# Scan operands of a four-layer image kernel: first pieces given inside the tick, later pieces one by one, last chunks' sums together

## The chip, the cores and the metric

The kernel runs on one core of a Trainium2 chip. The metric is the device time of one execution in microseconds (us); the lower, the better. Engines are named as in the profile: PE (TensorE matmul) and PEld (its weight load), DVE (VectorE), ACT (ScalarE), POOL (GpSimd) and SP (SyncE, which issues nearly all DMAs here). L12 is line 12 of the kernel before.

## The reference

`x` has the shape (4, 128, 64, 64): four images of 128 channels and 4096 pixels, float32. Four layers follow one another, each with a residual and a group norm of 32 groups in front:

```
x = x + attention(_gn(x))         # softmax attention over the 4096 pixels
x = x + radial_conv5x5(_gn(x))    # 128 -> 128 channels
x = x + selective_scan(_gn(x))    # the layer of this change
x = x + conv3x3(_gn(x))           # 128 -> 128 channels
```

The scan layer projects its input with Wx. It takes one half of the channels forwards and the other half backwards over the pixels. On each half it does:

```
xc    = silu(causal depthwise conv, 4 taps)
delta = softplus(xc @ Wd + bd);  Bm = xc @ WB;  Cm = xc @ WC
h[t]  = exp(delta[t] * A) * h[t-1] + (delta[t] * xc[t]) * Bm[t]    # 64 states per channel
y[t]  = sum over states(h[t] * Cm[t]) + D * xc[t]
```

The two halves are joined and projected with Wp.

## The kernel before

**Two streams in one order.** No scheduler moves instructions: each engine runs its instructions in the order in which the program gives them. One Python loop, `scan_core` (L1431), gives the recurrence in 1024 ticks: 256 for each of the four images, in four chunks of 1024 pixels, two directions, 16 groups of four states and two groups of channels. The other stream, `images` (L1781), is a chain of generators: load, attention, 5x5 convolution and scan operands of each image, and later the ends and the 3x3 convolutions. After each half tick the loop runs pieces of this second stream until the costs that they yield (0.7 for a `SLOT`, 0.86 for a `PRODUCT`) have used up the image's pace, so many units to a tick (`PACES`, L47). While image b is in the recurrence, the second stream makes image b+1. Before an image's first tick the loop runs the second stream without limit until the operands of its first chunk are there (`before`). For image 0 there is no recurrence to run beside, so its front stands alone.

**A tick.** In iteration i, POOL multiplies `db` for tick i+2 (`drive`, L1535), ACT makes the decay `da` of tick i+1 (`decay`, L1528), DVE scans tick i (`recur`, L1545), and the product with C, `hc`, is made on DVE (L1548) or for some ticks on POOL (`weigh`, L1566). `to_pool` gives POOL one product in three in the wide state, three of five while the operands of the next image are made ("operands" in `ready`), and one in five in the last part of that ("drives" in `ready`). PE adds the states up (L1584). SP loads the rows `br` and `cr` and the steps `dx` and `de` four ticks ahead, or up to eight at the start of an image.

**Wide and narrow.** Usually the decay of a tick is one instruction of 1024 elements into one of two double PSUM banks. While scan operands are made, these banks belong to the bank `s2` and three half banks. Decay and scan are then two instructions of 512 elements each. `widen` changes over when "narrow" is added to or taken from `ready`; the end of the 5x5 convolution adds it, the end of the scan operands takes it away.

**Scan operands of an image.** `Sums.settle` (L359) turns sums into scale and shift: small operations on DVE, and then two on POOL (L376, L377). In front of the scan it waits for the next tick (`next_tick`) before those two. `scan_prep` (L1240) clears the edges of the padded image `xn` on POOL (L1247, L1248), normalises its first and last piece of 512 pixels on ACT (`piece`, through L424), and hands over to `scan_operands` (L1263). That has a table of slots. For chunk i, at slot 5i + ...:

| slot | what | engine |
| --- | --- | --- |
| 0, 1 | `taps`: depthwise conv and Wx in 16 products (L1284) | PE |
| 4 | `halves`: half of it, and tanh (L1299, L1306; image 0 has the first on DVE, L1301) | ACT |
| 5 | `silu` (L1310), and the write of `xcd` | DVE, SP |
| 8, 9, 12 | `delta_product`, `row_product` 1 and 2 (L1319) | PE |
| 10 | `softplus`, its linear part (L1333, L1334) | ACT |
| 11, 13 | `row` 1 and 2: copies for B and C (L1325), and their writes | ACT, SP |
| 12 | `exp` (L1362, L1368) | ACT |
| 13 | `digits` (L1339, L1340) | DVE |

After chunk 3 and after chunk 7 (in image 0 after chunks 1, 5 and 7) come the logarithms of the chunks so far (`logs`, L1375), the additions that finish delta (`join`, L1347, and the write of `dd`), and delta times xc (`drives`, L1352, and the write of `dxd`). The additions run on POOL, or on DVE where the logarithm went to a PSUM bank: chunks 4, 5 and 6 of images 1 to 3. Slot 0 also normalises pieces 1 and 6, slot 1 pieces 2 and 5, slot 2 pieces 3 and 4. "read" at slot 2 lets the next image's load begin, ten turns later. After image 3's operands, `last_weights` (L917 to L920) prepares the weights of the last convolution on DVE.

**The next image beside it.** `both` runs an image's operands and the `start` of the image that follows it in turn, one piece of each. Its key products (`keys`, L477) begin after "taps" at slot 39.

Of the kernel before, what the change touches and what calls it, by code (L numbers as in the profile page):

```python
# [27 lines left out]
ALU = mybir.AluOpType  # L28
# [15 lines left out]


PRODUCT, VALUES, HOP, SLOT, AHEAD, EARLY = 0.86, 0.9, 1.7, 0.7, 4, 8
PACES = 2.60, 2.57, 2.57, 1.55  # L47


BQ, BK, BX, BP, CONVB, BD, DSKIP, MAINB, CONVW, ALOG = 0, 1, 2, 3, 4, 5, 6, 7, 8, 12  # L50
# [3 lines left out]
def conv_preact_kernel(  # L54
# [16 lines left out]
    nc = tc.nc  # L71
    B, C, H, W = x.shape
    L = H * W
# [7 lines left out]
    NM = L // MM  # L81
# [10 lines left out]
    pools, ready = {}, set()  # L92
    more = None

    def bank(tag, name):
        return pools.get(tag, ps).tile([P, MM], F32, tag=tag, name=name)
# [233 lines left out]
    class Sums:  # L330
# [25 lines left out]

            self.away, self.begun = other.minus, True

        def settle(self, name, wait=False):  # L359

            def cell(tag):
                return small.tile([P, 1], F32, tag=f"gn_{tag}", name=f"{tag}_{name}")

            total = small.tile([P, 2], F32, tag="gn_total", name=f"total_{name}")
            nc.vector.tensor_reduce(total, self.sums, AX.X, ALU.add)
            mean, power = self.spare[:, 0:1], self.spare[:, 1:2]
            nc.tensor.matmul(self.spare[:, 0:2], gmean, total, start=True, stop=True)
            off, less, var, rs, nb = (cell(tag) for tag in ("off", "less", "var", "rs", "nb"))
            minus = self.minus = small.tile([P, 1], F32, tag=f"gn_mi{name[0]}", name=f"mi_{name}")
            nc.vector.tensor_scalar(off, mean, self.away, -1.0, ALU.add, ALU.mult)  # L370
            nc.vector.scalar_tensor_tensor(less, mean, self.away, off, ALU.add, ALU.mult)
            nc.vector.scalar_tensor_tensor(var, less, GN_EPS, power, ALU.add, ALU.add)
            nc.vector.tensor_scalar(minus, mean, -1.0, None, ALU.mult)
            if wait:
                yield from next_tick()
            nc.gpsimd.tensor_tensor(rs, var, mhalf, ALU.pow)  # L376
            nc.gpsimd.tensor_tensor(nb, minus, rs, ALU.mult)  # L377
            return rs, nb

    def next_tick():  # L380

        begun = ticks_begun[0]
        while begun and ticks_begun[0] == begun:
            yield 0.4
# [38 lines left out]
    def normalise(dst, src, gn):  # L423
        nc.scalar.activation(dst, src, AF.Identity, scale=gn[0], bias=gn[1])  # L424
# [27 lines left out]
    def attention_start(b, xn):  # L452

        if b == 0:
            st = stats_tile(f"a{b}")
            for i in range(NM):
                nc.vector.bn_stats(st[:, i, :], xn[:, bass.ts(i, MM)])
                yield 0.0
            gn = yield from group_norm(st, f"a{b}")
        while b > 0 and (b - 1, "taps") not in ready:  # L460
            yield 0.0
        v = pools["big"].tile([P, VSIZE], F32, tag="V", name=f"v_{b}")
        v = v[:, : NJT * (C + 1)].rearrange("p (j c) -> p j c", c=C + 1)
        nc.gpsimd.memset(v[:, :, C : C + 1], 1.0)
        pvs = {}

        def piece(i):
            cut = bass.ts(i, L // 4)
            if b == 0:
                normalise(xn[:, cut], xn[:, cut], gn)  # L470

        def keys(i):

            tag = "saz"[i % 3] if b == 0 else "s" if i < 3 or i % 2 == 0 else "s2" if "s2" in pools else "z"
            pvs[i] = bank(tag, f"pv_{b}_{i}").rearrange("p (t c) -> p t c", c=C)
            for t in range(TPM):
                nc.tensor.matmul(  # L477
                    pvs[i][:, t, :], xn[:, bass.ts(i * TPM + t, P)], wv, start=True, stop=True
                )

        def take(i):
            nc.scalar.copy(v[:, i * TPM : (i + 1) * TPM, :C], pvs.pop(i))

        piece(0)
        yield SLOT
        for i in range(NM):
            if i % 2 == 0 and i // 2 + 1 < 4:
                piece(i // 2 + 1)
            keys(i)
            yield SLOT  # L490
            if b > 0:
                take(i)
                yield 0.0
            elif i > 0:
                take(i - 1)
        if b == 0:
            take(NM - 1)
        return xn, v
# [741 lines left out]
    def scan_prep(b, xs, st, mats4):  # L1240


        bc, dd, dxd, xcd, xsd = mats4
        pad = KC - 1
        gn = yield from st.settle(f"s{b}", True)
        xn = pools["big"].tile([P, VSIZE], F32, tag="V", name=f"xn2_{b}")
        nc.gpsimd.memset(xn[:, :pad], 0.0)  # L1247
        nc.gpsimd.memset(xn[:, pad + L : 2 * pad + L], 0.0)  # L1248

        def piece(*chunks):  # L1250
            for i in chunks:
                cut = slice(i * MM, (i + 1) * MM)
                normalise(xn[:, pad + cut.start : pad + cut.stop], xs[:, cut], gn)
            for i in {i // 2 for i in chunks if i % 2}:
                nc.sync.dma_start(xsd[:, bass.ts(i, CH)], xs[:, bass.ts(i, CH)])

        piece(0)
        piece(NM - 1)
        while "wide" in pools:
            yield HOP  # L1260
        return scan_operands(b, xn, mats4, piece)

    def scan_operands(b, xn, mats4, piece):  # L1263
# [78 lines left out]
        def join(c):  # L1342
            for i in range(c * CH // MM, (c + 1) * CH // MM):
                cut = bass.ts(i, MM)

                eng = nc.vector if b > 0 and NM // 2 <= i < NM - 1 else nc.gpsimd
                eng.tensor_tensor(delta[:, cut], delta[:, cut], us.pop(i), ALU.add)  # L1347
            nc.sync.dma_start(dd[c], delta[:, bass.ts(c, CH)])

# [20 lines left out]
        def logs(i, j):  # L1370
            for n in range(i, j):
                to = us[n]
                if b > 0 and j == NM and n - i < 3:
                    to = bank(("a", "z", "s2")[n - i], f"ln_{b}_{n}")
                nc.scalar.activation(to, us[n], AF.Ln)  # L1375
                us[n] = to

# [7 lines left out]
        def at(slot, f, *args):  # L1385
            slots.setdefault(slot, []).append((f, args))

        for i in range(NM):
            t = EVERY * i
            at(t, taps, i, 0, 1)  # L1390
            at(t + 1, taps, i, 2, 3)
            at(t + 4, halves, i)
            at(t + 5, silu, i)
            at(t + 8, delta_product, i)
            at(t + 9, row_product, i, 1)
            at(t + 10, softplus, i)
            at(t + 11, row, i, 1)
            at(t + 12, exp, i)
            at(t + 12, row_product, i, 2)
            at(t + 13, digits, i)  # L1400
            at(t + 13, row, i, 2)

        PER = CH // MM
# [1 line left out]
        for i, j in zip(cuts, cuts[1:]):  # L1405
            t = EVERY * (j - 1) + 15
            at(t, logs, i, j)
            for n, c in enumerate(range(i // PER, j // PER)):
                at(t + 1 + n, join, c)
                at(t + 3 + n, drives, c)  # L1410
                at(t + 4 + n, ready.add, (b, "operands", c))
        at(0, piece, 1, NM - 2)
        for n in range(2, NM // 2):
            at(n - 1, piece, n, NM - 1 - n)
        at(2, ready.add, (b, "read"))
        at(EVERY * (NM - 1) + 4, ready.add, (b, "taps"))
        at(EVERY * (NM - 1) + 13, ready.add, "drives")
        ready.add("operands")
        for t in range(max(slots) + 1):
            for f, args in slots.get(t, ()):  # L1420
                f(*args)
            yield SLOT
        ready.discard("operands")
        ready.discard("drives")
        ready.discard("narrow")
# [5 lines left out]
    def scan_core(mats4, ynds, before, widen, result):  # L1431
# [194 lines left out]
        def do(step, i, *args):  # L1626
            if 0 <= i < n:
                step(i, *args)

        for i in range(-AHEAD, n + 4):  # L1630
            if (i + AHEAD) % TICKS == 0 and i + AHEAD < n:
                before((i + AHEAD) // TICKS)
            do(drive, i + 2)
            ticks_begun[0] = i + AHEAD + 1 if i < n + 3 else 0
            do(keep, i - 1)
            late = i + 1 < n and i >= 0 and widen()
            if not late:
                do(decay, i + 1, 0)
            do(recur, i)
            if late:  # L1640
                do(keep, i)
                late()
                do(decay, i + 1, 0)
            do(weigh, i - 1)
            if i < n + 3:
                do(take, i - 4)
            do(preset, i - 4)
            do(collect, i - 3)
            yield i
# [20 lines left out]
    def program(safe):  # L1670
# [26 lines left out]
        def front(b, xn, v):  # L1697
# [21 lines left out]
            ynds[b] = dram.tile([NM, P, MM], F32, tag="ynd", bufs=B, name=f"ynd_{b}")  # L1719
            operands = yield from scan_prep(b, xs, st2, mats4[b])  # L1720
            if b + 1 < B:
                return (yield from both(operands, start(b + 1, 10)))
            yield from operands
            last_weights()

# [229 lines left out]
```

## Time and profile before

| | |
| --- | --- |
| time before, median of 3 runs | 4182.58 us (4182.18 to 4189.49) |
| the profiled execution | 4187.43 us |
| its span, first to last instruction | 4184.1 us |
| busy: PE, DVE, ACT, POOL | 3687.0, 3514.0, 2325.1, 3525.7 us |
| granted clock of PE, mean | 0.934 |
| first scan starts, last scan ends | 685.3 us, 4118.4 us |
| first scan of images 1, 2, 3 | 1559.4, 2429.4, 3307.8 us |
| narrow ticks | 0 to 7, 242 to 259, 497 to 514, 752 to 768 |

A busy engine in this table is busy over the whole span. A group's line in the profile gives its busy time, the mean of one instruction in ns, and the engine's idle time before such instructions with what ended it. A line of a timeline gives start, duration, engine, line, operation, output and inputs, and in square brackets the idle time before it. A line of the list of waits gives who waited for whom, the sum in us, the number of times and the longest.

### The profile page before, as it was taken

Reading aid. Unit: us, or ns where it says so; the run is one execution under the profiler, and the core shown is the slowest. Engines: PE = TensorE matmul, PEld = TensorE weight load, DVE = VectorE, ACT = ScalarE, POOL = GpSimd, SP = SyncE. Lnnn points to the kernel's source line nnn. Section 1 sums busy time; section 2 is a strip of 40 time slices with the busy share of each in tenths; the row PEclk is TensorE's granted clock in tenths of the full one; section 3 lists DMA queues with packets and bytes.
Section 4 is the critical chain, followed back from the end, with each engine's and each line's share of the span. In section 5 each row is a group of like instructions: output and inputs, shape, how many; then the busy total and the mean of one; then the engine's idle time right before and its main releaser. Section 6 shows DMA issues by size and latency. Waiting matters only on the chain. (4 is left out here: it accounts for less than half of the span.)

```text
span 4184.1 us, 49830 instructions
## 1 busy us (share of the span) xinstructions
PE 3687.0 (88%) x17668; PEld 2140.8 (51%) x17668; DVE 3514.0 (84%) x2441; ACT 2325.1 (56%) x3900; POOL 3525.7 (84%) x1688
## 2 busy tenths in 40 slices
PE   8999997999999979999999889999998576675856
PEld 4444443778875327887763368787733121221212
DVE  3842215999999979999999899999998899999996
ACT  3344306667665476766664676666645654545442
POOL 2433315999999979999999799999998899999995
PEclk9999998999999989999999999999999788797877
DMA  1020006555555666555555575555655756666661
GB/s 66 31 104 26 3 11 239 196 191 191 195 190 190 192 240 222 197 192 194 192 190 193 203 253 195 191 197 185 204 179 197 258 199 230 205 213 224 211 234 61
DMA packets 223728, 740.99 MB, mean 177 GB/s; under 512 B 29662, under 2 KB 30942, under 8 KB 223212
## 3 DMA queue, kind: packets, MB, share of 16 engines
q1 hardware_dynamic: 221548, 736.99, 52.0%
q8 instruction: 140, 2.29, 0.2%
q14 instruction: 120, 0.98, 0.1%
q10 hardware_dynamic: 1920, 0.73, 0.1%
HBM read 662.14 MB, written 75.47 MB: 176 GB/s over the span
## 5 line engine op out<-in xcount | busy, mean ns | idle before, releaser
L1535 POOL TENSOR_TENSOR db<-dx,br 128x1024 f32<-128x1024 f32 x1024 | 2398.5, 2367 | 119.4 <-DVE hc L1545 44.6
L1528 ACT ACTIVATE da<-de,a_neg 128x1024 f32<-128x1024 f32 (+1 forms) x1085 | 1160.3, 1070 | 375.2 <-DVE hc L1548 272.6
L1545 DVE TENSOR_TENSOR_SCAN da<-da,last,db 128x1024 f32<-128x1024 f32 (+1 forms) x500 | 1152.8, 2306 | 21.7 <-ACT last L1561 10.6
L1548 DVE TENSOR_TENSOR hc<-da,cr 128x1024 f32<-128x1024 f32 (+1 forms) x698 | 824.7, 1182 | 61.8 <-issue 1.3
L1566 POOL TENSOR_TENSOR hc<-hc,cr 128x1024 f32<-128x1024 f32 x354 | 837.4, 2366 | 6.8 <-ACT last L1561 3.6
L1584 PE MATMUL y<-hc,sel 128*32 128x512 f32 x4096 | 601.3, 649 | 270.2 <-POOL hc L1566 206.9
L748 PEld LDWEIGHTS acc<-v,exchange 128*128 128x128 f32 x6144 | 799.7, 191 | 48.3 <-issue 10.6
L727 PE MATMUL sc<-r,x 128*128 128x256 f32 x3072 | 803.0, 386 | 21.2 <-ACT exchange L740 16.2
L748 PE MATMUL acc<-v,exchange 128*128 128x129 f32 x6144 | 803.3, 275 | 1.5 <-ACT exchange L740 1.5
L727 PEld LDWEIGHTS sc<-r,x 128*128 128x128 f32 x3072 | 527.9, 191 | 188.5 <-ACT exchange L740 41.2
L1545 DVE TENSOR_TENSOR_SCAN hc<-da,last,db 128x1024 f32<-128x1024 f32 (+1 forms) x268 | 597.3, 2229 | 7.0 <-ACT last L1561 3.6
L740 ACT ACTIVATE exchange<-sc 128x512 f32<-128x512 f32 x768 | 441.8, 588 | 171.9 <-PE sc L727 164.6
L1584 PEld LDWEIGHTS y<-hc,sel 128*32 128x32 f32 x4096 | 113.6, 113 | 620.6 <-POOL hc L1566 303.4
L1545 DVE TENSOR_TENSOR_SCAN da<-da,db 128x1024 f32<-128x1024 f32 (+1 forms) x170 | 376.6, 2215 | 14.9 <-ACT da L1528 10.5
L1561 ACT COPY last<-da 128x1 f32<-128x1 f32 x511 | 80.4, 157 | 542.9 <-DVE hc L1548 541.9
L549 POOL TENSOR_TENSOR sidep<-sidep,exchange 128x512 f32<-128x512 f32 x120 | 165.0, 1375 | 254.3 <-ACT exchange L531 251.9
L531 ACT ACTIVATE exchange<-sc 128x512 f32<-128x512 f32 x256 | 152.6, 596 | 254.5 <-PE sc L530 246.5
L549 DVE TENSOR_TENSOR sided<-sided,exchange 128x512 f32<-128x512 f32 x120 | 98.5, 821 | 214.7 <-ACT exchange L531 213.6
L537 PE MATMUL acc<-exchange,v 128*128 128x512 f32 x512 | 261.9, 594 | 0.9
L530 PE MATMUL sc<-r,x 128*128 128x512 f32 x512 | 262.1, 594 | 0.6 <-ACT r L513 0.6
L893 PE MATMUL pcm<-xpm,cs 128*128 128x512 f32 x432 | 213.0, 643 | 10.3 <-ACT xpm L424 10.3
L1545 DVE TENSOR_TENSOR_SCAN hc<-da,db 128x1024 f32<-128x1024 f32 (+1 forms) x86 | 190.7, 2218 | 7.6 <-ACT da L1528 5.1
(295 smaller groups left out, 3048.6 us busy)
## 6 DMA issues: line engine op xcount, KB each, us to landing
br<-bm SPq DMA_DIRECT2D x512, 512.0 KB, 4.0
cr<-cm SPq DMA_DIRECT2D x512, 512.0 KB, 4.6
dx<-dxd SPq DMA_DIRECT2D x64, 512.0 KB, 5.3
de<-dd SPq DMA_DIRECT2D x64, 512.0 KB, 6.3
xs<-in_x_dram SPq DMA_DIRECT2D x16, 512.0 KB, 6.0
xsd<-xs SPq DMA_DIRECT2D x16, 512.0 KB, 5.2
xcd<-xc SPq DMA_DIRECT2D x16, 512.0 KB, 2.6
bm<-bs SPq DMA_DIRECT2D x32, 256.0 KB, 5.4
```

The lines of the kernel that those rows point to most:

```text
L530: nc.tensor.matmul(sc, xn[:, bass.ts(j, P)], rq[blk], start=True, stop=True)
L537: nc.tensor.matmul(acc[blk], v[:, j, :C], ring[:, u % NRING, :], start=j == 0, stop=j == NJT - 1)
L549: eng.tensor_tensor(s, s, ring[:, u % NRING, :], ALU.add)
L727: nc.tensor.matmul(sc[:, bass.ts(n, HM)], xn[:, bass.ts(2 * k + n, P)], rq[blk][:, cut], start=True, stop=True,)
L740: nc.scalar.activation(pt, sc, AF.Exp)
L748: nc.tensor.matmul(acc[part][:, bass.ts(t, CV)], ring[:, u % NRING, n * HM + t * P : n * HM + (t + 1) * P], v[:, 2 * k + n, :], start=(k, ...
L1528: nc.scalar.activation(da, rep["de", b, c, d, g][:, bass.ts(h, size)], AF.Exp, scale=a_neg[:, at(i)])
L1535: nc.gpsimd.tensor_tensor(dbs[i], rep["dx", b, c, d, g], rows["b", b, c, d, q], ALU.mult)
L1545: nc.vector.tensor_tensor_scan(h, da, db[:, cut], before, ALU.mult, ALU.add)
L1548: nc.vector.tensor_tensor(hc[:, cut], h, rows["c", b, c, d, q][:, cut], ALU.mult)
L1566: nc.gpsimd.tensor_tensor(hcs[i], hcs[i], rows["c", b, c, d, q], ALU.mult)
L1584: nc.tensor.matmul(y[r : r + SG, :], sel, hcs[first + gg][:, bass.ts(h, MM)], start=False, stop=q == NQ - 1, tile_position=(0, r), skip_gr ...
```

## The change

- `settle` takes a function instead of a flag. The two operations on POOL, and that function after them, are put on a list of hooks. The loop runs the list inside the next tick, behind its `drive` and ahead of its `decay` and `recur`. The function clears the edges of `xn` and normalises pieces 0 and 7. Without a running recurrence the list is run at once.
- The other six pieces get slots of their own: piece 1 at slot 2 and 6 at 3, 2 at 6 and 5 at 7, 3 at 11 and 4 at 12. "read" comes at slot 13 instead of 2, and the next image's load five turns after it instead of ten.
- `silu` moves from slot 5 to 6 of a chunk and `digits` from 13 to 14.
- At the last logarithms (slot 50), all additions are at slot 51, and the drives at 52 and 53. Slots after 50 yield no cost: there is one wait for the next tick after slot 50, and all that is left is given together.
- Two instead of three of the last logarithms go to PSUM banks (`a`, `z`; no longer `s2`), so chunk 6 is added on POOL. Odd key products use bank `s` while operands are made and `z` afterwards.
- The paces of images 1, 2 and 3 go from 2.57, 2.57, 1.55 to 2.56, 2.55, 1.53.

```diff
-PACES = 2.60, 2.57, 2.57, 1.55
+PACES = 2.60, 2.56, 2.55, 1.53
...
-        def settle(self, name, wait=False):
+        def settle(self, name, then=None):
...
-            if wait:
-                yield from next_tick()
-            nc.gpsimd.tensor_tensor(rs, var, mhalf, ALU.pow)
-            nc.gpsimd.tensor_tensor(nb, minus, rs, ALU.mult)
+
+            def finish():
+                nc.gpsimd.tensor_tensor(rs, var, mhalf, ALU.pow)
+                nc.gpsimd.tensor_tensor(nb, minus, rs, ALU.mult)
+                if then:
+                    then((rs, nb))
+
+            if then:
+                hooks.append(finish)
+                while hooks and ticks_begun[0]:
+                    yield 0.4
+                run_hooks()
+            else:
+                finish()
             return rs, nb
...
-            tag = "saz"[i % 3] if b == 0 else "s" if i < 3 or i % 2 == 0 else "s2" if "s2" in pools else "z"
+            tag = "saz"[i % 3] if b == 0 else "s" if i % 2 == 0 or "operands" in ready else "z"
...
-        piece(0)
-        piece(NM - 1)
+        def first(gn):
+            scale_shift.append(gn)
+            nc.gpsimd.memset(xn[:, :pad], 0.0)
+            nc.gpsimd.memset(xn[:, pad + L : 2 * pad + L], 0.0)
+            piece(0)
+            piece(NM - 1)
+
+        yield from st.settle(f"s{b}", first)
...
-                eng = nc.vector if b > 0 and NM // 2 <= i < NM - 1 else nc.gpsimd
+                eng = nc.vector if b > 0 and NM // 2 <= i < NM - 2 else nc.gpsimd
...
-                if b > 0 and j == NM and n - i < 3:
-                    to = bank(("a", "z", "s2")[n - i], f"ln_{b}_{n}")
+                if b > 0 and j == NM and n - i < 2:
+                    to = bank("az"[n - i], f"ln_{b}_{n}")
...
-            at(t + 5, silu, i)
+            at(t + 6, silu, i)
...
-            at(t + 13, digits, i)
+            at(t + 14, digits, i)
...
-                at(t + 1 + n, join, c)
-                at(t + 3 + n, drives, c)
-                at(t + 4 + n, ready.add, (b, "operands", c))
-        at(0, piece, 1, NM - 2)
-        for n in range(2, NM // 2):
-            at(n - 1, piece, n, NM - 1 - n)
-        at(2, ready.add, (b, "read"))
+                at(t + (1 if j == NM else 1 + n), join, c)
+                at(t + (2 if j == NM else 3) + n, drives, c)
+                at(t + (2 if j == NM else 4) + n, ready.add, (b, "operands", c))
+        for n in range(1, NM // 2):
+            at(EVERY * (n - 1) + 1 + (n == 1), piece, n)
+            at(EVERY * (n - 1) + 2 + (n == 1), piece, NM - 1 - n)
+        at(EVERY * (NM // 2 - 2) + 3, ready.add, (b, "read"))
...
-            yield SLOT
+            if t <= EVERY * (NM - 1) + 14:
+                yield SLOT
+            elif t == EVERY * (NM - 1) + 15:
+                yield from next_tick()
...
             ticks_begun[0] = i + AHEAD + 1 if i < n + 3 else 0
+            run_hooks()
             do(keep, i - 1)
...
-                return (yield from both(operands, start(b + 1, 10)))
+                return (yield from both(operands, start(b + 1, 5)))
```

More of the change, by code (lines that the diff above doesn't have):

```diff
@@ L373, in settle, with run_hooks @@
             nc.vector.tensor_scalar(minus, mean, -1.0, None, ALU.mult)
-            if wait:
-                yield from next_tick()
-            nc.gpsimd.tensor_tensor(rs, var, mhalf, ALU.pow)
-            nc.gpsimd.tensor_tensor(nb, minus, rs, ALU.mult)
+            def finish():
[10 more added lines that the diff above has]
+                finish()
             return rs, nb
+    hooks = []
+    def run_hooks():
+        while hooks:
+            hooks.pop(0)()
     def next_tick():
@@ L1244, in scan_prep @@
         pad = KC - 1
-        gn = yield from st.settle(f"s{b}", True)
         xn = pools["big"].tile([P, VSIZE], F32, tag="V", name=f"xn2_{b}")
-        nc.gpsimd.memset(xn[:, :pad], 0.0)
-        nc.gpsimd.memset(xn[:, pad + L : 2 * pad + L], 0.0)
+        scale_shift = []
         def piece(*chunks):
@@ L1252, in piece @@
                 cut = slice(i * MM, (i + 1) * MM)
-                normalise(xn[:, pad + cut.start : pad + cut.stop], xs[:, cut], gn)
+                normalise(xn[:, pad + cut.start : pad + cut.stop], xs[:, cut], scale_shift[0])
             for i in {i // 2 for i in chunks if i % 2}:
                 nc.sync.dma_start(xsd[:, bass.ts(i, CH)], xs[:, bass.ts(i, CH)])
-        piece(0)
-        piece(NM - 1)
+        def first(gn):
[5 more added lines that the diff above has]
+        yield from st.settle(f"s{b}", first)
         while "wide" in pools:
```

## The prediction

> **What bounds the kernel now.** I read the page's busy line and groups first, then the table of windows, then the timelines of ACT, DVE and POOL through the stretches that the change touches, then the list of waits.
>
> ```profile
> PE 3687.0 (88%) x17668; PEld 2140.8 (51%) x17668; DVE 3514.0 (84%) x2441; ACT 2325.1 (56%) x3900; POOL 3525.7 (84%) x1688
> ...
> L1535 POOL TENSOR_TENSOR db<-dx,br 128x1024 f32<-128x1024 f32 x1024 | 2398.5, 2367 | 119.4 <-DVE hc L1545 44.6 <-DMA dx<-dxd 27.4 <-DVE da L1545 17.2
> ```
>
> There are 1024 ticks, each with one POOL product of 2.367 us (L1535). Four windows compare nineteen ticks around each stage of scan operands (images 1, 2, 3) with nineteen steady ticks; the columns are microseconds, then busy time of PE, PEld, DVE, ACT and POOL.
>
> ```profile
> 1472.75:1578.67 105.92, 78.98 (x328) 31.44 (x327) 77.00 (x88) 79.58 (x132) 79.97 (x43) 0.85 0.70 240
> 2336.20:2439.80 103.60, 75.09 (x310) 32.00 (x311) 77.67 (x87) 78.93 (x131) 82.67 (x43) 0.84 0.69 248
> 3198.90:3311.70 112.80, 71.72 (x270) 22.57 (x262) 85.84 (x91) 76.11 (x124) 85.05 (x44) 0.80 0.65 240
> 1600.00:1659.60 59.60, 59.54 (x413) 48.37 (x412) 57.65 (x35) 40.79 (x73) 59.60 (x27) 1.00 0.54 186
> ```
>
> In steady ticks POOL is busy for all 59.60 us (3.14 a tick), and nothing that the change does reaches them. The three operand stages take 322.3 us where steady ticks would take 3 x 59.60 = 178.8, and no engine is busy for over 80 of 106 us there. The excess of 143.5 us is part work and part engines waiting for each other in order; the waiting is what the change can win or add to.
>
> **The change part by part.** Durations are those of the one profiled execution, 4187.43 us with a span of 4184.1; the median of the runs shown is 4182.58, 4.85 lower, and I take the same difference from both.
>
> *First pieces inside the tick.* ACT in image 1's stage:
>
> ```profile
> 1483.15 0.69 ACT L1528 ACTIVATE da<-de,a_neg 128x512 f32<-128x512 f32 x1 [5.23 <-DVE hc L1548]
> 1483.78 4.32 ACT L424 ACTIVATE xn<-xs,nb_s,rs_s 128x512 f32<-128x512 f32 x6
> 1488.00 0.67 ACT L1528 ACTIVATE da<-de,a_neg 128x512 f32<-128x512 f32 x1
> ...
> 1496.03 0.69 ACT L1299 ACTIVATE xc<-pt,hbias 128x512 f32<-128x512 f32 x1 [2.96 <-PE pt L1284]
> ```
>
> ACT is idle for 5.23 us, then six normalisations stand between the two halves of one decay, and DVE's second half scan pays 3.48 us:
>
> ```profile
> 1488.70 1.28 DVE L1545 TENSOR_TENSOR_SCAN hc<-da,hc,db 128x512 f32<-128x512 f32 x1 [3.48 <-ACT da L1528]
> 1491.87 0.69 DVE L1310 SCALAR_TENSOR_TENSOR xc<-pt,xc 128x512 f32<-128x512 f32 x1 [1.88 <-ACT pt L1306]
> ```
>
> POOL's scale and shift are done at 1480.64 (L377 starts 1480.45, 0.19). In the hook, the two memsets and pieces 0 and 7 follow at once: two normalisations at 0.72 end near 1482.2, inside ACT's idle 5.23. The hook's POOL instructions stay behind the same drive, and POOL waits 1.17 us for DVE after them, so they cost nothing; without that wait they would cost their 0.9. Pieces 1, 6, 2, 5, 3, 4 go to slots 2, 3, 6, 7, 11, 12, behind the second half of the decay. The second half scan then starts 3.5 us earlier. The next scan (1492.48) stands behind the silu of chunk 0, which needs the taps. They began at 1484.72, took until 1490.5, and can begin at 1482.2: 2.5 us earlier. The four normalisations left over, 2.9 us, must then run where ACT waited 2.96 us for PE. Per stage the gain is between 0 (ACT full later) and 3.5; I take 2.5, as that wait covers them: 3 x 2.5 = **-7.5**. SP gets the four writes of xs (0.4 to 0.6 each to issue) spread over slots 0 to 11, each for data long there. The next image's load moves from slot 12 to about 18, six slots or 1.6 ticks. It lands in 6.4 us and its first reader waits for slot 39, 5.7 ticks off: nothing; without that distance the key products would start up to 6 us late.
>
> *Silu and digits a slot later.* Both are DVE instructions in front of which DVE waits for ACT. The list of waits for image 1's stage:
>
> ```profile
> DVE pb L1339 <- ACT u L1368: 9.5, 3, 6.2
> ...
> DVE xc L1310 <- ACT pt L1306: 4.4, 3, 1.9
> ```
>
> Images 2 and 3 have 4.4 and 4.8 for L1339, and 5.4 and 8.1 for L1310. That is 36.6 us over 48 instructions, 0.76 each. A slot costs 0.7 of 2.57 units a tick, 0.27 tick, so about 13 of the 48 move past the next tick's scan, which can use the wait: 9.9 us. PE's product waits for the silu, and the softplus on ACT for that product; moved past a scan (2.6 us) they come later, so I keep half: **-5** (from -10 to +5, if the later products hold ACT up as long as DVE is freed).
>
> *Last sums together.* Before, the last four logarithms were followed in the same half tick by three additions on DVE:
>
> ```profile
> 1569.17 1.88 DVE L1347 TENSOR_TENSOR exchange<-exchange,ln 128x512 f32<-128x512 f32 x3 [7.13 <-ACT ln L1375]
> ```
>
> Of those 7.13 us, 6.11 were ACT's decay waiting for the transfer of de, so at most 1 us goes here, and images 2 and 3 have no such wait at this place. Now the additions come after the next scan. One moves from DVE (0.68) to POOL (1.27), and POOL gets 2 x 1.27 + 2 x 2.37 = 7.3 us in one run before its next drive. The scans have two drives in hand, 5 to 8 us, which mostly covers the run. Without this cover it would cost up to 6. SP holds two dd and two dxd writes behind it, and row loads queue behind those. I take **+3** for three stages, from -1 to +18 (6.1 us each, the wait for de in image 1).
>
> The weights of the last convolution (L917) follow the sums in image 3. POOL:
>
> ```profile
> 3298.94 2.36 POOL L1535 TENSOR_TENSOR db<-dx,br 128x1024 f32<-128x1024 f32 x1
> 3301.24 2.35 POOL L1566 TENSOR_TENSOR hc<-hc,cr 128x1024 f32<-128x1024 f32 x1
> 3303.53 2.37 POOL L1535 TENSOR_TENSOR db<-dx,br 128x1024 f32<-128x1024 f32 x1
> ```
>
> and on DVE in the same microseconds
>
> ```profile
> 3299.37 6.94 DVE L917 TENSOR_TENSOR cs<-cs 128x384 f32<-128x384 f32 x1
> 3306.35 0.36 DVE L918 TENSOR_SCALAR cs<-cs 128x384 f32<-128x384 f32 x1
> ```
>
> L917 takes 6.94 us where its neighbour on as many columns takes 0.36, and ends 0.4 us after POOL's run. It stands behind a POOL run after the change too, so I take 0, from -6 to +4 (a run 9.6 to 12 long, less the 1.4 of the additions ahead of it). The Trainium skill's page "SBUF — State Buffer", section "Who interferes with whom", says that a VectorE instruction with two SBUF inputs takes a port that GpSimd's reads use too, and that whoever comes second is blocked for a whole instruction. The trace agrees in that 6.94 covers three POOL instructions. By that rule the new run of joins and drives would hold L917 for its whole length, and the sum would be 3 us higher.
>
> *Wide banks sooner.* The tail's slots 50 to 55 cost 4.2 units, 1.6 ticks. Now it waits for the next tick, so the narrow stretch ends about one tick sooner. DVE's narrow tick is 2 x 1.28 + 2 x 0.69 = 3.94 against 2.31 + 1.18 = 3.49 wide: 0.45 x 4 images = **-1.8** (0 to -4).
>
> *The rest.* Logarithm banks, key banks and paces. Image 1's key products waited 11.5 us for the additions that hold the third bank, but no scan waited for them: 0. The pace of 1.53 for 1.55 delays the last background work by 1.3% of some 236 ticks, 3 ticks; it is now done by tick 1003 of 1024: 0, and up to 10 us if it were not. In image 0 DVE's copy of the second row now goes ahead of the digits, which saves 0.45 us a chunk where its product is ready and costs 1.4 where it is late (DVE waited 1.8 us for it at 668.81). With twelve group norm stops moved against the ticks I call all of it 0, from -6 to +6.
>
> Sum: -7.5 - 5 + 3 - 1.8 = -11.3. The profiled execution would take 4176.1, the median 4171.3.
>
> **The rivals.** *ACT is the stage's real bound.* It is busy for 79.6 of 105.9 us, more than DVE, and the normalisations and decays are the same in number. Then what is hidden at the start comes back a few ticks later, the slot's delay moves waits from DVE to ACT, and only the 1.8 and about 2 of the first term stay: 4178.8, no change. For it speaks that ACT runs with gaps of 0.4 to 1.6 us through ticks 244 to 249; against it that every stage has some 27 us of ACT idle.
>
> *The tail becomes the stall (slower).* In image 1 POOL waited 4.93 us for dx and ACT 6.11 for de, both loads issued behind other transfers on SP. If SP's writes behind the 7.3 us run hold the row loads for longer than they have in hand (four ticks of 3.14 less 4.6 to land, 8 us), each stage pays about 6.1; with the drive of 2.36 and a weighing of 2.35 ahead, the run is 12 us, past that point. With L917 at +4, silu and digits giving nothing and the other terms as above: -7.5 - 1.8 + 18.3 + 4 = +13, 4195.6. Against it: in images 2 and 3 the same transfers were no long wait.
>
> *More is freed.* Digits of chunk 4 waited 6.2 us in image 1 behind four logarithms and two table loads. Moved past a scan there, and the other two terms at their better ends: -10.5 - 10 - 1 - 4 = -25.5, 4157.1.
>
> **How the numbers follow.** Forecast 0.54, ACT bound 0.14, the tail 0.20, more freed 0.12. A measurement of this kernel can tell about 0.2%, 8.4 us, from no change. The forecast's own range is 4162 to 4178; a tenth of it lies within 8.4 us. So faster is 0.49 + 0.12 = 0.61, within the bound 0.05 + 0.14 = 0.19, slower 0.20. A range from 4153 to 4193 leaves out the farther half of the tail's case and a little of the best.
>
> **What would show it.** Right: two normalisations ahead of the first half decay at each switch, no wait of 3.48 us in the scan after it, taps 2.5 us earlier; DVE's waits at L1310 and L1339 together under 30 us; narrow scans one tick fewer a stage; the nineteen ticks of each stage shorter by 2 to 6 us. Wrong: waits for dx, de or cr over 5 us in all three stages, POOL's drive late after the sums, L917 over 9 us, or stages of the old length with more ACT busy time in them.

## Result and the profile after

The changed kernel takes 4177.45 us (median of 22 runs, 4172.68 to 4182.07), the kernel before 4185.65 in the same number of runs (4181.68 to 4189.68). The ratio is 0.9981 with an interval of 0.9975 to 0.9988: some 8 us faster (5.0 to 10.5), a little less than the 8.4 us that was called the bound, but with an interval that stays clear of zero. The profiled execution took 4180.85 us, its span 4179.0.

The page's busy line and its first group, after:

```profile
PE 3697.7 (88%) x17668; PEld 2145.1 (51%) x17668; DVE 3515.0 (84%) x2436; ACT 2327.7 (56%) x3896; POOL 3523.3 (84%) x1688
...
L1558 POOL TENSOR_TENSOR db<-dx,br 128x1024 f32<-128x1024 f32 x1024 | 2399.6, 2367 | 107.7 <-DMA dx<-dxd 29.9
```

No engine's busy time fell by more than 2.4 us (POOL's); POOL's idle time ahead of the products is 11.7 us less (107.7 against 119.4). The table of windows, nineteen ticks around each operand stage, from the tick ahead of the one in which the sums are settled:

```profile
1473.54:1573.97 100.43, 80.87 (x320) 33.72 (x320) 77.00 (x87) 80.82 (x134) 81.35 (x44) 0.86 0.70 252
2330.11:2432.56 102.45, 79.54 (x315) 33.16 (x316) 77.28 (x88) 80.67 (x132) 82.91 (x44) 0.87 0.73 262
3192.88:3305.80 112.92, 74.75 (x270) 22.70 (x262) 89.86 (x91) 75.46 (x121) 86.22 (x45) 0.82 0.71 250
```

They sum up to 315.80 us, before 322.3: 6.5 less, 5.5 of them in image 1 and none in image 3, where DVE is busy for 4 us longer. With the ticks ahead of them and behind them (36 ticks a stage, 234 to 270, 489 to 525 and 744 to 780) the sums are 484.49 against 486.25: only 1.8 less. So part of what is won inside a stage is lost around it. How much is not the same in every execution: in a second one of the changed kernel (e5 below) the nineteen ticks sum up to 311.3 and the 36 to 479.5, 6.7 less than before.

From the start of the first scan to that of the last, the changed kernel is 7.2 us shorter, so in this execution most of the gain lies outside the stages, where the prediction let the change reach nothing: ticks 525 to 744 take 4.3 us less (4.3 in e5 too), ticks 270 to 489 2.8 less (0.9 in e5) and the last ones 1.0 less (0.3), while those ahead of 234 take 2.6 more (3.0). In the seven kernels below with the new tail, ticks 525 to 744 lose 12.8 to 15.2 us against steady ticks, in the seven with the old one 15.2 to 17.4. So this part seems to go with the tail. With the tail alone (e9), though, ticks 270 to 489 lose 3.5 us more than before, and how the ticks between the stages get shorter or longer was not looked into.

**What came as it should.** ACT, DVE and POOL at image 3's switch, with waits in brackets:

```profile
3200.74 0.10 POOL L1274 MEMSET xn<- 128x3 f32 x1
3200.80 1.52 ACT L440 ACTIVATE xn<-xs,nb_s,rs_s 128x512 f32<-128x512 f32 x2 [2.76 <-POOL xn L1274]
...
3203.28 1.30 ACT L1551 ACTIVATE da<-de,a_neg 128x512 f32<-128x512 f32 x2 [0.96 <-DVE hc L1571]
3204.07 1.28 DVE L1568 TENSOR_TENSOR_SCAN hc<-da,last,db 128x512 f32<-128x512 f32 x1 [0.89 <-ACT da L1551]
...
3205.46 1.28 DVE L1568 TENSOR_TENSOR_SCAN hc<-da,hc,db 128x512 f32<-128x512 f32 x1
```

The two normalisations lie where ACT had been idle, the two half decays follow each other, and the second half scan (the last line) has no bracket: the wait of 3.48 us, which all three images had before, is gone. From the reduction of the sums (L365) to the first silu it is 10.1, 10.2 and 11.8 us, before 13.9, 14.0 and 14.4.

**What was lost again.** The list of waits over image 1's 36 ticks, after (who waited for whom, sum, times, longest):

```profile
DVE da L1568 <- ACT da L1551: 9.7, 6, 4.3
...
DVE hc L1568 <- ACT da L1551: 7.2, 3, 4.3
...
POOL db L1558 <- DMA dx<-dxd: 3.5, 1, 3.5
...
DVE pb L1359 <- ACT u L1388: 3.5, 4, 1.6
...
DVE xc L1330 <- ACT pt L1326: 3.1, 4, 1.6
```

DVE waits less in front of silu and digits: 24.6 us in the three stages, before 36.6. But its scans wait more for decays on ACT: 43.8 us, before 29.0. (In e5 the two sums are 26.4 and 37.8.) The longest at the end of image 1's stage:

```profile
1564.48 0.59 ACT L498 COPY v<-pv 128x512 f32<-128x512 f32 x1 [1.57 <-PE pv L493]
...
1566.46 0.59 ACT L498 COPY v<-pv 128x512 f32<-128x512 f32 x1 [1.39 <-PE pv L493]
...
1569.22 0.69 ACT L529 ACTIVATE r<-pr,bqk 128x512 f32<-128x512 f32 x1 [2.17 <-PE pr L527]
1569.80 0.68 ACT L1551 ACTIVATE da<-de,a_neg 128x512 f32<-128x512 f32 x1
...
1570.52 1.30 DVE L1568 TENSOR_TENSOR_SCAN da<-da,da,db 128x512 f32<-128x512 f32 x1 [4.30 <-ACT da L1551]
```

Two copies and a query of the next image stand ahead of the decay on ACT and wait 5.1 us for PE; the scan pays 4.30.

### The profile page after: what moved, and what is told of

Its sections match the earlier page's. It is cut to its first block, busy times and chain, and to the rows that moved or that the text cites. A ratio compares the mean times of both kernels' runs of the same rounds, so it can differ in the third digit from the quotient of the medians.

```text
span 4179.0 us, 49812 instructions
## 1 busy us (share of the span) xinstructions
PE 3697.7 (88%) x17668; PEld 2145.1 (51%) x17668; DVE 3515.0 (84%) x2436; ACT 2327.7 (56%) x3896; POOL 3523.3 (84%) x1688
## 3 DMA queue, kind: packets, MB, share of 16 engines
q1 hardware_dynamic: 221548, 736.99, 52.7%
## 5 line engine op out<-in xcount | busy, mean ns | idle before, releaser
L1558 POOL TENSOR_TENSOR db<-dx,br 128x1024 f32<-128x1024 f32 x1024 | 2399.6, 2367 | 107.7 <-DMA dx<-dxd 29.9
L1568 DVE TENSOR_TENSOR_SCAN da<-da,last,db 128x1024 f32<-128x1024 f32 (+1 forms) x502 | 1153.3, 2297 | 26.4 <-POOL db L1558 9.9
L743 PE MATMUL sc<-r,x 128*128 128x256 f32 x3072 | 806.8, 388 | 15.9 <-ACT exchange L756 10.2
L565 DVE TENSOR_TENSOR sided<-sided,exchange 128x512 f32<-128x512 f32 x120 | 98.3, 819 | 214.5 <-ACT exchange L547 213.5
L909 PE MATMUL pcm<-xpm,cs 128*128 128x512 f32 x432 | 214.3, 646 | 10.4 <-ACT last L1584 7.5
```

The lines of the kernel that those rows point to most:

```text
L565: eng.tensor_tensor(s, s, ring[:, u % NRING, :], ALU.add)
L743: nc.tensor.matmul(sc[:, bass.ts(n, HM)], xn[:, bass.ts(2 * k + n, P)], rq[blk][:, cut], start=True, stop=True,)
L1558: nc.gpsimd.tensor_tensor(dbs[i], rep["dx", b, c, d, g], rows["b", b, c, d, q], ALU.mult)
L1568: nc.vector.tensor_tensor_scan(h, da, db[:, cut], before, ALU.mult, ALU.add)
```

## Experiments

"Loss" below is the time of a stretch of ticks over 3.137 us for each (a steady tick: 59.60 us by 19), read from the start of each scan in one profiled execution. Two executions of the same kernel (the changed one) differ by 1.9 us in the whole recurrence, and by up to 2.9 in one stage, so smaller differences between two profiles say nothing. "us" is the ratio times 4186, with its interval.

| kernel | time | ratio | us | loss in stages 1, 2, 3 | all ticks |
| --- | --- | --- | --- | --- | --- |
| before | 4185.65 | 1 | 0 | 49.3, 45.4, 52.7 | 221.6 |
| changed | 4177.45 | 0.9981 (0.9975 to 0.9988) | -8.0 (-10.5 to -5.0) | 45.4, 47.5, 52.8 | 214.3 |
| e5 changed, run again | 4178.38 | 0.9979 (0.9970 to 0.9988) | -8.8 (-12.6 to -5.0) | 43.4, 47.5, 49.9 | 212.4 |
| e1 first pieces alone | 4180.10 | 0.9985 (0.9976 to 0.9994) | -6.3 (-10.0 to -2.5) | 48.2, 44.0, 49.5 | 214.4 |
| e10 silu and digits alone | 4181.19 | 0.9988 (0.9979 to 0.9997) | -5.0 (-8.8 to -1.3) | 49.7, 45.3, 51.0 | 217.9 |
| e9 tail alone | 4176.91 | 0.9981 (0.9972 to 0.9990) | -8.0 (-11.7 to -4.2) | 43.6, 44.7, 49.3 | 213.3 |
| e6 paces alone | 4187.07 | 1.0002 (0.9993 to 1.0011) | +0.8 (-2.9 to +4.6) | 50.7, 49.2, 54.7 | 223.7 |
| e2 changed, old tail | 4176.26 | 0.9976 (0.9966 to 0.9986) | -10.0 (-14.2 to -5.9) | 46.4, 44.5, 50.1 | 215.7 |
| e3 changed, old slots | 4173.53 | 0.9966 (0.9952 to 0.9979) | -14.2 (-20.1 to -8.8) | 43.9, 48.0, 51.9 | 212.2 |
| e4 changed, weights late | 4170.36 | 0.9961 (0.9948 to 0.9975) | -16.3 (-21.8 to -10.5) | 42.6, 47.8, 40.6 | 206.0 |
| e7 old slots, weights late | 4172.53 | 0.9965 (0.9952 to 0.9979) | -14.7 (-20.1 to -8.8) | 43.9, 48.4, 43.4 | 205.6 |
| e8 one SBUF input | 4175.83 | 0.9978 (0.9969 to 0.9987) | -9.2 (-13.0 to -5.4) | 42.6, 47.9, 51.8 | 214.5 |
| e11 before, weights late | 4179.13 | 0.9986 (0.9977 to 0.9995) | -5.9 (-9.6 to -2.1) | 51.2, 45.5, 45.6 | 213.3 |
| e12 first pieces, weights late | 4172.96 | 0.9969 (0.9957 to 0.9981) | -13.0 (-18.0 to -8.0) | 50.5, 43.9, 42.6 | 209.2 |

**e1, first pieces alone.** On the kernel before: the hook in `settle`, the pieces at slots of their own, and the shorter lag of the next image's load.

```diff
-        gn = yield from st.settle(f"s{b}", True)
+        yield from st.settle(f"s{b}", first)
...
-        at(0, piece, 1, NM - 2)
+            at(EVERY * (n - 1) + 1 + (n == 1), piece, n)
```

> The kernel before with the first pieces alone: scale, shift and pieces 0 and 7 in the hook, the other six one by one in their slots, the load's slots with them. Theory 1 (the stages won at their start and lost it again in the new tail): as the tail is the old one here, the 4 to 8 us that each stage is ahead at its third tick in the trace of the changed kernel stay, and this kernel beats it: 15 us under before, some 4170. Theory 2 (ACT bounds the stage, what is hidden at the start comes back): each stage ends as before, 4183 to 4186. Theory 3 (the paces made the gain, between the stages): no gain either, 4185.

It gave -6.3 us. By the third tick after the settling, its stages had lost 9.1, 10.5 and 10.3 us, before 12.6, 13.0 and 13.4: 2.5 to 3.5 us a stage won at the start, 9.1 in all, of which 5.7 are left at the stages' ends. None of the three cases fits: there is a gain, but nothing like the 15 us of the first.

**e2 and e3, one part taken out of the changed kernel.** e2 has the old tail (sums, drives, slot costs, three PSUM banks for logarithms), e3 the old slots.

```diff
-                at(t + (1 if j == NM else 1 + n), join, c)
-                at(t + (2 if j == NM else 3) + n, drives, c)
+                at(t + 1 + n, join, c)
+                at(t + 3 + n, drives, c)
```

> The changed kernel with the old tail: additions and drives one slot after the other, every slot at its cost, three logarithms in PSUM banks, chunk 6 added on DVE. Theory 1: the new tail costs 5 us in each of images 2 and 3 and nothing in image 1 by the traces (ticks 14 to 20 of the stage), so this kernel is 10 us under the changed one, 4168. Theory 2: the stage's length is set by ACT, the tail moves nothing: 4177 within 3. Theory 3: the paces fit the short tail, and with a longer one the next stage comes 1.5 ticks later; nothing within 3 us, 4177.

```diff
-            at(t + 6, silu, i)
+            at(t + 5, silu, i)
...
-            at(t + 14, digits, i)
+            at(t + 13, digits, i)
```

> The changed kernel with silu and digits in their old slots (5 and 13). By the prediction's term of 5 us it is slower by 5: 4182. By the traces (between the third and the twelfth tick the stages lose 21.7, 22.4 and 26.4 us before, 22.0, 24.2 and 23.3 after) the slots do nothing: 4177 within 2.

Neither is slower than the changed kernel. By the ratios e3 is 5 to 6 us below it and e2 1 to 2, both within the intervals. So in the changed kernel neither the tail nor the later slots show a gain of their own, and the intervals leave out both the 10 us that the old tail was to win there and the 5 us that the old slots were to lose.

**e4, weights of the last convolution late.** The four instructions of `last_weights` on DVE go behind the recurrence.

```diff
             yield from operands
-            last_weights()
...
             for _ in work:
                 pass
+            last_weights()
```

> The changed kernel with the weights of the last convolution made after the recurrence, where DVE and POOL are idle, instead of right after image 3's operands. If the 10.38 us of that one DVE instruction stood in the path, image 3's stage loses 45 instead of 53 us and the kernel takes 7 us less: 4170. If POOL's run of additions, drives and a product set the end of it anyway, only POOL's idle 5.3 us behind it can go: 4173. If the tail waits for ACT there, nothing: 4177.

It has the lowest time of all, as the first of its cases said: 4170.36 us (4166.48 to 4173.23). The first of the four behind the recurrence, with POOL at rest:

```profile
4103.24 0.55 DVE L933 TENSOR_TENSOR cs<-cs 128x384 f32<-128x384 f32 x1
```

The other three take 0.36, 0.56 and 0.56 us there, the four 2.03. In image 3's tail of the changed kernel they take 11.86, beside a POOL run:

```profile
3283.33 2.55 POOL L1367 TENSOR_TENSOR exchange<-exchange,u 128x512 f32<-128x512 f32 x2
...
3285.09 10.38 DVE L933 TENSOR_TENSOR cs<-cs 128x384 f32<-128x384 f32 x1
3285.77 4.69 POOL L1372 TENSOR_TENSOR xc<-exchange,xc 128x1024 f32<-128x1024 f32 x2
3290.36 2.40 POOL L1558 TENSOR_TENSOR db<-dx,br 128x1024 f32<-128x1024 f32 x1
3292.66 2.40 POOL L1589 TENSOR_TENSOR hc<-hc,cr 128x1024 f32<-128x1024 f32 x1
3295.51 0.36 DVE L934 TENSOR_SCALAR cs<-cs 128x384 f32<-128x384 f32 x1
...
3300.32 2.35 POOL L1558 TENSOR_TENSOR db<-dx,br 128x1024 f32<-128x1024 f32 x1 [5.26 <-DVE da L1568]
```

L933 ends 0.4 us behind POOL's run, and POOL then stands idle for 5.26 us, as the scans it waits for stood behind L933. Stage 3 loses 40.6 us in e4, 52.8 in the changed kernel.

**e5, the changed kernel again.**

```diff
 (no edit)
```

> The changed kernel once more, as the measure for the others of this batch: 8 us under the kernel before. A second trace of the same instructions shows how far a stage's loss moves by itself; up to now 45.4, 47.5 and 52.8 us.

Time and ratio agree. But its profiled execution has another picture in the same place:

```profile
3282.77 2.51 POOL L1367 TENSOR_TENSOR exchange<-exchange,u 128x512 f32<-128x512 f32 x2
...
3285.36 0.55 DVE L933 TENSOR_TENSOR cs<-cs 128x384 f32<-128x384 f32 x1
3285.52 5.01 POOL L1372 TENSOR_TENSOR xc<-exchange,xc 128x1024 f32<-128x1024 f32 x2 [0.24 <-DVE exchange L1367]
3285.95 2.38 DVE L934 TENSOR_SCALAR cs<-cs 128x384 f32<-128x384 f32 x1
3288.36 2.59 DVE L935 SCALAR_TENSOR_TENSOR cs<-cs 128x384 f32<-128x384 f32 x1
3290.48 2.67 POOL L1558 TENSOR_TENSOR db<-dx,br 128x1024 f32<-128x1024 f32 x1
3290.98 2.58 DVE L936 SCALAR_TENSOR_TENSOR cs<-cs 128x384 f32<-128x384 f32 x1
```

Here L933 starts 0.1 us after POOL's additions (L1367) have ended and finds POOL free, and each of the other three takes about as long as one POOL instruction; the four need 8.1 us. In the first execution L933 started while the second of POOL's additions still ran. The other traces go the same way. Where the first of the four began with POOL idle (e5, e3, e9), the two engines took turns. Where it began inside a POOL instruction that another followed without a gap (before, changed, e1, e2, e6, e10), it lasted to the end of POOL's run, 6.7 to 10.4 us.

**e6, paces alone.**

```diff
-PACES = 2.60, 2.57, 2.57, 1.55
+PACES = 2.60, 2.56, 2.55, 1.53
```

> The kernel before with the new paces alone (2.56, 2.55, 1.53). If first pieces and weights explain the whole, nothing: within 2 us of the kernel before. If the paces made the 7 us that the traces show between the stages (ticks 270 to 744), 5 to 7 us less.

By time nothing that can be told, as called. But in its profile image 2's stage loses 3.8 us more than before, and more than that in its tail: from the fourteenth tick after the settling of the sums to the twentieth it loses 15.5 us, before 7.8. So the paces are not neutral inside a stage.

**e7, old slots and late weights** in the changed kernel (the edits of e3 and e4).

```diff
-            at(t + 6, silu, i)
+            at(t + 5, silu, i)
...
-            last_weights()
```

> The changed kernel with silu and digits in their old slots and the weights made after the recurrence. If the slots' 4 us and the weights' 8 us add up: 12 us under the changed kernel, 20 under the one before. If the slots' 4 us were chance: 8 under the changed kernel, 16 under the one before.

With -14.7 us it is no faster than e3 (-14.2) or e4 (-16.3) by time, although its profiled execution lost 6.6 us less than e3's. Three kernels lie here within their intervals; which of them is best is open.

**e8, one SBUF input for the long addition.** ACT first copies one of the two inputs of L933 to a PSUM bank (a new line, so that the four stand at L935 to L938).

```diff
+        other = bank("s", "m3_other")[:, : 3 * C].rearrange("p (k c) -> p k c", c=C)
+        nc.scalar.copy(other, m3[:, 6:9, :])
-        nc.vector.tensor_tensor(half, m3[:, 0:3, :], m3[:, 6:9, :], ALU.add)
+        nc.vector.tensor_tensor(half, m3[:, 0:3, :], other, ALU.add)
```

> The changed kernel with the weights in their place, but one of the two inputs of the long addition copied to PSUM by ACT first, so that DVE reads one input from SBUF. If DVE stood there for a second SBUF input while POOL worked, the addition takes 0.4 to 0.5 us instead of 10.38, image 3's stage loses 41 to 44 us instead of 53, and the kernel is 6 to 8 us under the changed one. If DVE waited for anything else (the loaded weights, a place in its queue), it stays at some 10 us and nothing is won. ACT's copy, 0.5 us, is extra.

```profile
3283.95 0.55 DVE L935 TENSOR_TENSOR cs<-cs,m_other 128x384 f32<-128x384 f32 x1
3284.53 9.50 DVE L936 TENSOR_SCALAR cs<-cs 128x384 f32<-128x384 f32 x1
...
3291.44 2.37 POOL L1591 TENSOR_TENSOR hc<-hc,cr 128x1024 f32<-128x1024 f32 x1
```

The addition takes 0.55 us beside POOL's additions, but the wait moves to the instruction behind it, which has one input, in SBUF: 9.50 us, up to the end of POOL's run at 3293.8. Freeing one of the four shows no gain: -9.2 us against -8.0 and -8.8, and stage 3 loses 51.8.

**e9 and e10, the tail alone and the slots alone**, each on the kernel before (e9 has the changed banks of the logarithms too, but not those of the key products).

```diff
-                at(t + 1 + n, join, c)
-                at(t + 3 + n, drives, c)
+                at(t + (1 if j == NM else 1 + n), join, c)
+                at(t + (2 if j == NM else 3) + n, drives, c)
...
+            elif t == EVERY * (NM - 1) + 15:
+                yield from next_tick()
```

> The kernel before with the new tail alone (one wait, additions and drives together, two logarithms in PSUM banks). The traces so far have image 2's stage 3 us longer with the new tail (47.5 to 48.4 against 44.0 to 45.4 lost) and the ticks 270 to 744 outside the stages 4 us shorter (24 to 29 against 30 to 31). If both hold here, they cancel: within 3 us of the kernel before. By the prediction's term: 3 us slower. If the tail is what makes the whole faster than the first pieces alone: 3 us faster.

```diff
-            at(t + 5, silu, i)
+            at(t + 6, silu, i)
...
-            at(t + 13, digits, i)
+            at(t + 14, digits, i)
```

> The kernel before with silu and digits a slot later and nothing else. By the prediction's term 5 us faster. By the two runs with the old slots on the changed kernel (4 us faster once, nothing once) between nothing and 4 us slower.

The tail alone gains 8.0 us where the prediction's terms made a loss of 1.2 (3 less 1.8), and the slots alone gain the 5 that were called. Two lines of e10's list of waits over image 1's stage, with the old tail, show waits that are gone with the new tail:

```profile
DVE exchange L1347 <- ACT ln L1375: 6.6, 1, 6.6
...
ACT da L1528 <- DMA de<-dd: 5.4, 1, 5.4
```

All seven kernels with the old tail have both in image 1: 4.6 to 7.1 us for the logarithm and 3.9 to 6.1 for `de`. None of the seven with the new tail has the first, and only e5 has a little of the second, 1.8 us. Stage 1 loses 43.6 us in e9, 49.3 before.

**e11 and e12, late weights without the change, and with the first pieces alone.** e11 is the edit of e4 on the kernel before, e12 that and the edit of e1.

```diff
             yield from operands
-            last_weights()
```

> The kernel before with the weights of the last convolution made after the recurrence. The four DVE instructions stand 8.4 us there before and 11.9 in the changed kernel's first trace. If all of their time is in the path, 7 to 8 us faster than before; if POOL's idle 4.6 us behind them is what counts, 4 to 5.

> The kernel before with the first pieces of the change and the weights made after the recurrence, old tail, old slots, old paces. If these two are all that matters, their gains add up: 6 and 8, 14 us faster than before, as fast as the changed kernel with late weights (16). If tail, slots or paces give a share, some 10 us faster at most.

The late weights give -5.9 us on the kernel before, with stage 3 at 45.6 instead of 52.7. With the first pieces they give -13.0, and -6.3 and -5.9 make -12.2: these two add up.

## Why the prediction was right, and where it was not

It gave 4171.3 us, 11.3 below the kernel before; 8.0 were measured. As a time, 4177.45 is nearer to the 4178.8 of the rival in which ACT is the bound, since the kernel before came out 3.1 us higher than the 4182.58 that the sum started from. The direction and the range held. But one term was far off, the adding up seems to have failed as well, and their errors went opposite ways: that the sum came within 3.3 us is in good part luck.

- **First pieces, -7.5.** Measured alone: -6.3 (e1). Each sign came: the normalisations ahead of the half decays, no wait of 3.48, the taps 3.1 to 3.4 us earlier after the reduction of the sums (2.5 were called), the first silu 2.6 to 3.8.
- **Silu and digits, -5.** Measured alone: -5.0, from -8.8 to -1.3 (e10). The number fits, but the mechanism isn't shown. DVE's waits there fell from 36.6 to 24.6 us as called (under 30), and to 25.9 in e10. But the scans' waits for decays on ACT rose from 29.0 to 39.6 in e10, so by its trace nearly all was given back and not half, and its three stages are only 1.4 us shorter in sum. In the changed kernel it is the same: from e3 to it, DVE's waits at silu and digits go from 37.0 to 24.6 us, and the scans' waits for ACT from 34.3 to 43.8 (26.4 and 37.8 in e5).
- **Last sums together, +3, and wide sooner, -1.8.** Measured together: -8.0 (e9). Narrow ticks fell from 61 to 57 as called. The term was mis-sized, and the step that failed is "Of those 7.13 us, 6.11 were ACT's decay waiting for the transfer of de, so at most 1 us goes here". That wait was taken as given from outside, but it goes away with the tail, and DVE's with it; image 1's stage loses 43.6 us in e9, before 49.3. What does it was not separated: the order of the sums, the one wait for the next tick, or that the stage then begins a tick earlier (image 1's sums are reduced in tick 239 in all seven kernels with the new tail, in tick 240 in the seven others). The rival in which the tail becomes the stall fell: POOL's wait for dx is 3.5 us in image 1, less than the 4.93 before, and images 2 and 3 have none.
- **L917, 0.** Its change was small, as said: the four instructions went from 8.4 us to 11.9 in one execution and 8.1 in another. The prediction said that the trace agrees with the rule of the Trainium skill's page "SBUF — State Buffer", section "Who interferes with whom", by which the second one waits for a whole instruction; but 6.94 us covered three POOL instructions, not one. What the prediction made of it, a wait for the whole run, is the row of 10.38 in the first execution; the second comes nearer to the page. L917 over 9 us was named as a sign of a wrong forecast; it came once, and the time held all the same. What the prediction missed is that the wait needn't be there: moved away, the four are worth about 6 to 8 us (e11, e4), as much as the change.
- **The rest, 0.** The paces gave +0.8, from -2.9 to +4.6 (e6).
- **The steady ticks, nothing.** The sentence that nothing which the change does reaches them doesn't hold in the traces: ticks 525 to 744 are 4.3 us shorter in both executions.
- **The sum.** The measured parts make -6.3 - 5.0 - 8.0 + 0.8 = -18.5, and all of them together give -8.0. The half intervals of the four, squared, summed and rooted, give 7.5, so -26 to -11, which only just misses the -10.5 to -5.0 of the change and meets the -12.6 to -5.0 of e5. So it is likely, not certain, that the terms don't add up, which the prediction did as if each had its own microseconds. Two parts may still add up: with the paces' 0.8, first pieces and slots -10.0 (e2) for -10.5, first pieces and tail -14.2 (e3) for -13.5, both with wide intervals. The tail and the slots without the first pieces were not run.

Where the gain of the stages goes can be followed, why only in part. The table has the losses against steady ticks in images 1, 2 and 3, first up to the third tick after the settling of the sums, then from the fourteenth tick after it to the twentieth, and DVE's waits in front of scans for decays on ACT in these last ticks.

| kernel | to the third tick | fourteenth to twentieth | scans' waits for ACT there |
| --- | --- | --- | --- |
| before | 12.6, 13.0, 13.4 | 13.5, 7.8, 11.5 | 0, 3.3, 1.3 |
| changed | 5.8, 4.7, 8.9 | 13.2, 12.7, 16.5 | 8.6, 8.7, 2.6 |
| e5 changed, run again | 7.5, 4.7, 8.9 | 12.5, 12.7, 12.7 | 5.7, 8.7, 2.6 |
| e9 tail alone | 9.4, 10.4, 11.2 | 7.8, 9.5, 10.0 | 4.2, 6.1, 1.2 |

So the changed kernel's stages are 4.5 to 8.3 us ahead by the third tick. In their tails image 1's then lacks what the tail wins by itself, and image 2's loses about 5 us of the lead. In both, most of it is scans that wait for decays on ACT. In image 3 such waits are short; there the difference is mostly the four instructions for the weights (without them, in e4, these ticks lose 4.7). The waits for ACT are the mechanism of the rival in which ACT is the bound, and the gain lies between that rival's 3.8 us and the forecast. It is no lack of ACT's time: ACT is busy for 80.8 of 100.4 us in image 1. It is the order, work that waits for PE ahead of a decay that could run. One could blame the new bank of the odd key products for the 5.1 us ahead of the decay in image 1, since e9, with the old bank, has 2.5 there; but e5, with the new one, has 2.0.

What sets these waits, and which pair of edits clashes, stays open, and one rival was not run: the paces. They move the second stream against the ticks, and all kernels with both first pieces and the new tail have the new ones. Image 2's tail loses 7.8 to 8.0 us in the five kernels with the old paces and the old tail and 9.5 in e9, but 12.7 to 15.5 in all eight with the new paces, e6 among them, where nothing else is changed. Against it: in e6 these ticks hold a wait of 4.4 us for a logarithm and no longer waits for decays than before, and image 2's sums come a tick later there, so it is not quite the same work. The changed kernel with the old paces would tell. Of the three stages, image 1's got 5.5 us shorter in the nineteen ticks, within the 2 to 6 that were called; image 2's got 1.2 and image 3's nothing (e5: 7.0, 1.2 and 2.8).

## What to carry to other kernels

Where engines run their instructions in a fixed order and wait for each other, price the parts of a change one by one, but don't count on their sum: a microsecond won at the start of a stage counts only if nothing later in the same stage takes it, so follow it to the stage's end. A short VectorE instruction with a duration far above that of its neighbours, ending with GpSimd's run, should be moved to where GpSimd rests, all the instructions of its kind with it; here four instructions of 2.0 us in all cost about 6 to 8. And a wait that looks like a transfer's may belong to the order of the program around it: see whether it is there in every stage. Last, two profiles of one kernel can differ by some us in a stage, so take a second one before you rest a reading on a small difference.

## What the runs showed of the hardware

VectorE instructions on 384 columns that took 0.36 to 0.56 us with GpSimd idle took 2.4 to 2.6 or 6.7 to 10.4 us while GpSimd ran elementwise instructions back to back. The Trainium skill's page "SBUF — State Buffer", section "Who interferes with whom", names among the VectorE instructions that contend with GpSimd those with two SBUF inputs, where GpSimd reads SBUF, and `tensor_scalar` in its two-port modes, and lets the second to issue wait for the whole instruction of the first. The traces agree on the kinds: L933 with both inputs in SBUF (10.38), an in-place `tensor_scalar` (9.50 in e8, 2.38 in e5), and 0.55 for the addition with one input in PSUM. They differ on the length: VectorE waited for GpSimd's whole run, up to five instructions, in the changed kernel and in e8, and for about one instruction each in e5, the same kernel as the former. GpSimd pays too in the second picture: its product for the scan took 2.67 us there, 2.40 in the first. In the nine traces that have the four instructions unchanged beside GpSimd's work, the engines took turns in the three where the first of them began with GpSimd idle, and VectorE waited for the whole run in the six where it began inside a GpSimd instruction. Why it is so, no run here shows.
